# Running sums for neighbour ranks, a 16-bit un-permute, and norms on GpSimd, in a four-layer graph kernel

## The chip, the cores and the metric

One core of one Trainium2 chip runs the whole program in one launch. The metric is device time in microseconds, the median of the runs; less is better. Five engines work side by side, each with its own instruction stream in program order, held together by semaphores: TensorE (PE in the profile, its weight loads PEld), VectorE (DVE), ScalarE (ACT), GpSimd (POOL) and SyncE (SP), which here issues the DMAs of the main part.

## The reference, cut to what matters

There are 32 graphs of 512 nodes with 64 features. Four layers follow each other, and each is `x = layernorm(x + layer(x))`.

```python
x = _layernorm(x + _L0_gnn_ref(x, adj))                       # A x / clip(deg, 1)
x = _layernorm(x + _L1_gnn_ref(x, adj, weight, bias))         # Chebyshev polynomials of the Laplacian, 4 orders
x = _layernorm(x + _L2_gnn_ref(x, adj, att_W, att_b))         # hyperbolic attention over all pairs of nodes
x = _layernorm(x + _L3_gnn_ref(x, adj, nodemask, W1, b1, W2, b2))
```

Layer 3 is what the change touches most. It thins out each node's neighbour list, takes for each node and feature three interpolated quantiles (0.25, 0.5, 0.75) over the node's neighbours, and puts the weighted sum of them through a two-layer perceptron:

```python
vals = jnp.where(valid[..., None], x[:, None, :, :], big)
sv = jnp.sort(vals, axis=2)
for tau, wt in zip(TAUS, QWEIGHTS):
    q = gather(lo) * (1.0 - frac) + gather(hi) * frac         # at rank tau * (m - 1)
    agg = agg + wt * q
y = relu((x + agg) @ W1 + b1) @ W2 + b2
```

`_layernorm` divides by `sqrt(var + 1e-5)` over the 64 features and has no scale or offset of its own.

## The kernel before, in words

A graph's 512 nodes lie on 128 partitions times T = 4 blocks. Each graph passes through lanes, and each lane has its own buffers and PSUM banks (`BANKS`, L513: two for pairs, one for each of the others that it names).

- `front` (L882) loads the adjacency, transposes it to `AT`, and computes layers 0 and 1. The degree gives `deg`, `dc`, `dm`, `dsc` and `pos` (L913 to L932), columns of 128x4 numbers; `dsc` scales every `y` that is multiplied by the adjacency.
- `pairs` (L969) is layer 2's arithmetic over all pairs of nodes; its second half, from L1094, is the lane `tail`, which ends in the norm after layer 2 and in `x3h`, the result split into three bfloat16 parts.
- `stage_graph` (L878) finds the thinned neighbour matrix `V` and then, in `order` (L830), sorts the nodes by their number of neighbours. `rk` is a node's place, `perm` a one-hot matrix of it, and `VP` the permuted neighbour matrix in four blocks. `slot` says which number a neighbour has in a node's list. It is a prefix sum over nodes: block j needs a triangular product with its own block and a product with a matrix of twos for every earlier block, ten products in all. Four more, with ones, give the counts.
- `gather` (L1147) turns slots into one-hot matrices `oh` on VectorE and multiplies them with `x3h`, so that each neighbour's features land in their slot. Before this, GpSimd pads the unused columns of the sorting areas `SB` and `SH` (L1157). `SB` holds the body (nodes with fewer neighbours) and `SH` the head (the 64 nodes of two graphs with most).
- `sort` (L1239) runs a sorting network of minima and maxima over `SB` on VectorE, weights the sorted values and adds them up in the PSUM bank `PA`; `ap` is the result, for two graphs together.
- `head` (L1270) does the same for `SH`, and calls `finish` (L1315) for each graph of a pair. `finish` puts the nodes back in their old order: `PT`, one-hot in fp32, times `ap` in fp32, four products a graph of 64 columns of weights and 512 moving columns. `dense` (L1346) is the perceptron and the last norm. For the last pair, `spots` (L1296) prepares the one-hot matrices beforehand.

Every norm is `layernorm` (L725). VectorE takes statistics of each block (`bn_stats`, then `bn_aggr`) and adds the epsilon, GpSimd raises to the power -0.5 (`rsqrt`, L719), VectorE forms the offset, and ScalarE applies scale and offset.

Nothing runs in the order of the code. The class `Order` (L181) records every operation with an engine, a cost, its buffers and what it depends on; `issue` (L295) then plays the operations through in planned time and writes out one instruction order for each engine. An operation's due time comes from its lane's window in `STAGES` (L1415), in units of one graph's period: a lane with (2.7, 2.9) is due 2.7 periods after the graph's turn. Costs are numbers in the code: a small GpSimd operation counts 1.0 us and 0.5 us until its result is seen (L468), `rsqrt` 0.8 and 0.6 (L722). TensorE stays with one class of matmul shape unless another class is due more than `STAY` = 51 us earlier (L188). Where the plan leaves TensorE idle for more than 0.3 us, it puts in filler matmuls on zeros or on constants (`stay_active`, L1451). Once written, the order is fixed, and an instruction that waits holds all that stands behind it on its engine.

The groups of the profile carry the helper's line: 448 is `tt`, 452 `ts`, 455 `stt`, 458 `cp`, 471 and 475 the GpSimd helpers, 483 `act`, 502 `mm`, 507 `tr`. Tile names carry the lane in front.

Of the kernel before, what the change touches and what calls it, by code (L numbers as in the profile page):

```python
# [8 lines left out]
F32 = mybir.dt.float32  # L9
# [11 lines left out]
P = 128  # L21
EPS = 1e-5
# [158 lines left out]
class Order:  # L181
# [6 lines left out]
    STAY = 51.0  # L188
# [215 lines left out]
def tile_adj_resnorm(ctx: ExitStack, tc: tile.TileContext, x, adj, nodemask, w1k, b1k, att_w, att_b,  # L404
# [61 lines left out]
    def gp(f, out, ins):  # L466

        seq.op("POOL", 1.0, 0.5, f, [out], ins)  # L468
# [142 lines left out]
    onesb = const.tile([P, P], BF16, name="onesb")  # L611
    nc.vector.memset(onesb, 1.0)
    zero = const.tile([P, 2 * P], BF16, name="zero")
# [105 lines left out]
    def rsqrt(v, name):  # L719

        y = col(name)
        seq.op("POOL", 0.8, 0.6, lambda: nc.gpsimd.tensor_tensor(y, v, mhalf, op=OP.pow), [y], [v])  # L722
        return y

    def layernorm(dst, z):  # L725

        st = seq.tile(pools["small"], [P, T, nc.vector.BN_STATS_DIM], F32, "st", 2)
# [102 lines left out]
    def order(b, res):  # L830
# [18 lines left out]
        cp(rkh, rk)  # L849
# [9 lines left out]
        slot = seq.tile(pools["keep"], [P, T, N], F16, "slot", 2)  # L859
        for j in range(T):  # L860
            pt = bank()
            for k in range(j + 1):
                mm(pt, UC[:, :P] if k == j else UC[:, P:2 * P], VP[:, k, :], start=(k == 0), stop=(k == j))
            act(slot[:, j, :], pt, AF.Copy)
        pt = bank()
        for k in range(T):
            mm(pt, onesP, VP[:, k, :], start=(k == 0), stop=(k == T - 1))
# [14 lines left out]
    def front(b, res):  # L882
# [39 lines left out]
        layernorm(R[:, :, :D], z)  # L922
# [3 lines left out]
        ts(dm, deg, 2e-35, None, op0=OP.max)  # L926
        dsc = rsqrt(dm, "dsc")
        pos = col("pos")
        ts(pos, deg, 0.0, None, op0=OP.is_gt)
        tt(dsc, dsc, pos, op=OP.mult)  # L930
# [23 lines left out]
        for t in range(T):  # L954
            mm(pt[:, t, :], onesb, bias1, start=True, stop=False)
            for u in range(nu):
                mm(pt[:, t, :], RT[:, u, t * P:(t + 1) * P], wk[:, u, :], start=False, stop=(u == nu - 1))

        FL = FLS[:, b % 2]
        var, rs = layernorm(FL[:, :, :D], pt[:, :, :D])  # L960
# [8 lines left out]
    def pairs(b, res):  # L969
# [129 lines left out]
        stt(s1, q, -2.0, s1, op0=OP.mult, op1=OP.add)  # L1099
        tt(s1, s1, hh, op=OP.mult)  # L1100
# [169 lines left out]
    def head(b, res):  # L1270
# [21 lines left out]
        act(ap[P - CUT:, :, 1, :], pt[P - CUT:, :2 * P].rearrange("p (g c) -> p g c", g=2), AF.Copy)  # L1292
        for g in range(2):
            finish(b - 1 + g, res["ends"][g], ap[:, g], res["spots"][g] if b == B - 1 else None)

    def spots(ends):  # L1296
# [4 lines left out]
        ones = [seq.tile(mid, [P, 4, N], F32, f"ones{g}", 1, tag) for g, tag in enumerate(("EX", "RW"))]  # L1301
# [13 lines left out]
    def finish(b, end, ap, spot):  # L1315
        rk, x3 = end
        if spot:
            ones, home = spot
            po = bank(home=home and "pairs")
            for u in range(2):  # L1320
                for h in range(2):
                    mm(po[h * D:(h + 1) * D, :], ap[:, u, h * D:(h + 1) * D], ones[:, 2 * h + u], start=(u == 0),
                       stop=(u == 1 and h == 1), pair=True)
# [11 lines left out]
        for u in range(2):  # L1335
            PT = seq.tile(pools["fin"], [P, 2, N], F32, "PT", 1)
            for h in range(2):
                onehot(PT[:, h, :], rr, nposc[:, 2 * h + u:2 * h + u + 1], pools["fin"])
            for h in range(2):
                mm(po[h * D:(h + 1) * D, :], ap[:, u, h * D:(h + 1) * D], PT[:, h, :], start=(u == 0),  # L1340
                   stop=(u == 1 and h == 1), pair=True)
# [4 lines left out]
    def dense(po, x3T, x3, dst, nm, home=None):  # L1346
# [14 lines left out]
        for t in range(T):  # L1361
            mm(py[:, t, :], onesb, bias2, start=True, stop=False)
# [8 lines left out]
    limits = const.tile([B, 2, K + 1], F32, name="limits")  # L1371
# [12 lines left out]
    def within_bounds():  # L1384
# [17 lines left out]
        for i, op in enumerate((OP.is_gt, OP.is_lt)):  # L1402
# [12 lines left out]
    STAGES = {"front": (-0.6, -0.5), "pairs": (1.2, 1.3), "tail": (0.2, 1.5), "graph": (0.9, 1.0), "gather": (2.7, 2.9),  # L1415
              "sort": (4.5, 4.6), "head": (4.7, 5.6), "ends": (4.0, 4.5), "check": (3.4, 4.8)}

    nc.scalar.preload_act_table_set("natural_log_exp_and_others")
    with ExitStack() as fast:
# [31 lines left out]
        def stay_active():  # L1451
            if seq.open:
                return nc.tensor.matmul(PA[:, 2 * P:], zero[:, :P], zero, start=False, stop=False)  # L1453
# [251 lines left out]
```

## Time and profile before

| | |
|---|---|
| median of 3 runs | 2621.71 us (2621.48 to 2628.53) |
| the profiled execution | 2622.02 us, span 2620.2 us |
| mean granted TensorE clock | 0.982 |
| busy: PE, DVE, ACT, POOL | 2458.2, 2402.7, 1879.2, 815.8 us |
| DMA | 49.96 MB, 19 GB/s on average |

The span runs from the first instruction to the last. An engine counts as busy while at least one of its instructions runs, register, semaphore and DMA-issuing instructions left out. A line of a group reads: source line, engine, operation, output and inputs by name, shape, count, then busy time in us and the mean of one in ns, then the idle time ahead of the group's instructions and what ended it. A line of waits reads: who waited, for whom, us in total, times, the longest. Matmuls overlap, and their ends are modelled, so that a TensorE which is 94% busy may still have room.

### The profile page before, as it was taken

What the parts mean: (1) busy time and instruction counts of PE and PEld (TensorE: products, weight loads), DVE (VectorE), ACT (ScalarE), POOL (GpSimd) and SP (SyncE); (2) the same over time, 40 slices, a digit from 0 to 9 for tenths busy, and PEclk for the clock granted to TensorE, in tenths of its full rate; (3) what the DMA queues carried; (4) which work ended last, traced back from release to release, by engine and by line L of the source; (5) the groups of instructions that cost most, each with busy time, mean ns of one, the idle gap of its engine ahead of it and who ended that gap; (6) DMA issues with size and microseconds to landing.
All of it is one profiled execution on the core that took longest, in us unless ns stands there. A gap on an engine that the chain in (4) does not pass through costs nothing.

```text
span 2620.2 us, 55667 instructions
## 1 busy us (share of the span) xinstructions
PE 2458.2 (94%) x19641; PEld 1635.4 (62%) x19667; DVE 2402.7 (92%) x9002; ACT 1879.2 (72%) x4406; POOL 815.8 (31%) x1783
## 2 busy tenths in 40 slices
PE   7999999999999999999999999999999999999997
PEld 6666566666666666666656666566666666666655
DVE  3668998999999999999999999999999999998996
ACT  5666677767777777767777677777777778776761
POOL 1233332332343333322333233333323333332210
PEclk9999999999999999999999899999999999998999
DMA  1100000000000000000000000000000000000000
GB/s 38 33 23 21 17 14 15 25 22 23 18 11 22 20 25 21 24 17 13 20 21 25 19 19 13 20 23 22 26 19 13 18 19 26 19 11 3 5 7 8
DMA packets 119723, 49.96 MB, mean 19 GB/s; under 512 B 53740, under 2 KB 119436, under 8 KB 119436
## 3 DMA queue, kind: packets, MB, share of 16 engines
q1 hardware_dynamic: 118272, 46.15, 6.4%
q8 instruction: 156, 2.56, 0.4%
q14 instruction: 131, 1.07, 0.1%
q10 hardware_dynamic: 1164, 0.18, 0.0%
HBM read 37.93 MB, written 8.39 MB: 18 GB/s over the span
## 4 chain that ended last, share of the span: by engine, by line
DVE 72%; PE 18%; ACT 6%; issue 2%; POOL 2%; DMA 0%; ACTq 0%; DVEq 0%
DVE SB L448 17%; DVE SH L448 8%; DVE gather_oh L452 6%; PE front_bank L502 5%; DVE pairs_Q L448 4%; PE gather_bank L502 3%; PE graph_bank L502 3%; DVE pairs_RW L448 3%; PE pairs_bank L502 3%; DVE sort_prod L448 3%; DVE pairs_Wt L455 3%; DVE pairs_L L455 2%; DVE tail_v L448 2%; DVE pairs_EX L448 2%; DVE pairs_RW L455 2%
## 5 line engine op out<-in xcount | busy, mean ns | idle before, releaser
L448 DVE TENSOR_TENSOR SB<-SB 128x448 f32<-128x448 f32 (+11 forms) x1424 | 565.8, 424 | 12.2 <-ACT SB L483 0.7
L502 PE MATMUL gather_bank<-gather_oh,tail_x3h 128*64 128x448 f16 (+5 forms) x5376 | 516.5, 321 | 4.8 <-ACT SB L483 3.4
L502 PEld LDWEIGHTS <-tail_x3h 128*64 128x64 bf16 x5376 | 296.0, 111 | 214.3 <-issue 112.8
L448 DVE TENSOR_TENSOR SH<-SH 128x32 f32<-128x32 f32 (+11 forms) x1744 | 347.4, 246 | 8.1
L502 PE MATMUL pairs_bank<-pairs_FT 67*128 67x512 f32 (+7 forms) x768 | 316.9, 516 | 18.7 <-ACT pairs_EX L483 7.1
L452 DVE TENSOR_SCALAR gather_oh<-graph_slot 128x256 f16<-128x256 f16 (+9 forms) x864 | 252.3, 337 | 25.3 <-PE gather_bank L502 23.5
L502 PE MATMUL front_bank<-front_AT,front_y 128*64 128x512 f32 x768 | 189.5, 607 | 18.5 <-DVE front_y L448 17.0
L502 PEld LDWEIGHTS pairs_bank<-pairs_FT 67*128 67x128 f32 (+1 forms) x768 | 130.2, 194 | 83.2 <-issue 19.7
L502 PE MATMUL graph_bank<-graph_perm,graph_V 128*128 128x512 f16 x512 | 141.0, 382 | 16.1 <-DVE graph_perm L452 13.8
L502 PEld LDWEIGHTS <-graph_nbT 128*128 128x128 f16 x1536 | 113.1, 99 | 57.6 <-issue 17.3
L722 POOL TENSOR_TENSOR front_rs<-front_var,mhalf 128x4 f32<-128x4 f32 x64 | 83.4, 1303 | 201.8 <-DVE front_var L452 152.9
L502 PEld LDWEIGHTS front_bank<-XA,front_AT 128*128 128x128 f32 x1024 | 126.0, 194 | 13.6 <-issue 6.3
L1453 PE MATMUL PA<-zero 128*128 128x256 bf16 x973 | 132.9, 278 | 0.1
L502 PE MATMUL pairs_bank<-FLS,pairs_Wt 128*128 128x66 f32 x1024 | 124.7, 274 | 3.9 <-DVE pairs_Wt L455 3.8
L502 PEld LDWEIGHTS pairs_bank<-FLS,pairs_Wt 128*128 128x128 f32 x1024 | 120.6, 192 | 10.9 <-DVE pairs_Wt L455 7.8
L502 PE MATMUL front_bank<-XA,front_AT 128*128 128x65 f32 x1024 | 124.5, 274 | 0.0
L448 DVE TENSOR_TENSOR pairs_RW<-pairs_RW,pairs_EX 128x640 f32<-128x640 f32 x128 | 104.1, 815 | 18.7 <-ACT pairs_RW L483 18.4
L502 PEld LDWEIGHTS <-tabs 128*128 128x128 f16 x1296 | 78.3, 100 | 64.2 <-issue 54.9
L502 PEld LDWEIGHTS front_bank<-front_AT,front_y 128*64 128x64 f32 x768 | 54.5, 137 | 95.6 <-issue 63.0
L483 ACT ACTIVATE graph_VP<-graph_bank 128x512 f16<-128x512 f32 x128 | 75.5, 590 | 53.7 <-PE graph_bank L502 49.4
L483 ACT ACTIVATE SB<-gather_bank 128x448 f32<-128x448 f32 (+2 forms) x192 | 81.3, 438 | 43.4 <-PE gather_bank L502 43.0
L502 PE MATMUL head_bank<-head_PT,sort_ap 128*64 128x512 f32 x240 | 111.2, 608 | 0.1
(354 smaller groups left out, 6569.8 us busy)
## 6 DMA issues: line engine op xcount, KB each, us to landing
front_A<-in_adj_dram SPq DMA_DIRECT2D x128, 256.0 KB, 2.7
XA<-in_x_dram SPq DMA_DIRECT2D x32, 128.0 KB, 2.2
xs<-tail_x SPq DMA_DIRECT2D x32, 128.0 KB, 1.9
out_dram<-head_zo SPq DMA_DIRECT2D x31, 128.0 KB, 2.0
out_dram<-tail_ends SPq DMA_DIRECT2D x1, 128.0 KB, 2.1
wk<-in_L_gnn_weight_dram ACTq DMA_DIRECT2D x1, 64.0 KB, 3.0
w1s<-in_L_gnn_W_dram ACTq DMA_DIRECT2D x2, 32.0 KB, 2.0
attw<-in_L_gnn_att_W_dram ACTq DMA_DIRECT2D x2, 0.2 KB, 3.2
```

What stands on the lines that cost most here:

```text
L448: vec(lambda: nc.vector.tensor_tensor(out, a, b, op=op), out, [a, b])
L452: vec(lambda: nc.vector.tensor_scalar(out, a, s1, s2, op0=op0, **kw), out, [a], True, (s1, s2))
L455: vec(lambda: nc.vector.scalar_tensor_tensor(out, a, s, b, op0=op0, op1=op1), out, [a, b], False, (s,))
L483: 0.3, lambda: nc.scalar.activation(out, a, f, scale=scale, **kw), [out, accum_out], [a, after] + sc, table)
L502: return nc.tensor.matmul(out, w, a, start=start, stop=stop)
L722: seq.op("POOL", 0.8, 0.6, lambda: nc.gpsimd.tensor_tensor(y, v, mhalf, op=OP.pow), [y], [v])
L1453: return nc.tensor.matmul(PA[:, 2 * P:], zero[:, :P], zero, start=False, stop=False)
```

## The change

Four things are edited. The prefix sum keeps a running sum of the blocks of `VP` on VectorE, so that each later block needs two products and the counts one. `ap` is split into three bfloat16 parts `aph`, and the one-hot matrices of `finish` and `spots` become half precision. The norms of the lanes tail and head, and small column operations (`rkh`, `dm`, `pos`, `dsc`, `s1`), go to GpSimd; the norms of the front lane keep their form (`soon=True`). The ordering's numbers change: costs of GpSimd operations, `STAY`, `STAGES`. Besides, `onesP` takes the place of `onesb`, the filler on zeros reads its moving operand from one column, and `limits` is half precision.

```diff
-    STAY = 51.0
+    STAY = 70.0
...
-        seq.op("POOL", 1.0, 0.5, f, [out], ins)
+        seq.op("POOL", 0.28, 0.25, f, [out], ins)
...
-    onesb = const.tile([P, P], BF16, name="onesb")
-    nc.vector.memset(onesb, 1.0)
-    zero = const.tile([P, 2 * P], BF16, name="zero")
+    zero = const.tile([P, P], BF16, name="zero")
...
-        seq.op("POOL", 0.8, 0.6, lambda: nc.gpsimd.tensor_tensor(y, v, mhalf, op=OP.pow), [y], [v])
+        seq.op("POOL", 1.1, 0.3, lambda: nc.gpsimd.tensor_tensor(y, v, mhalf, op=OP.pow), [y], [v])
...
-    def layernorm(dst, z):
+    def layernorm(dst, z, soon=False):
+        if not soon:
+            st = seq.tile(pools["small"], [P, T, nc.vector.BN_STATS_DIM], F32, "st", 2)
+            for t in range(T):
+                bn_stats(st[:, t, :], z[:, t, :])
+            off, even, var, d, odd, v = (st[:, :, i] for i in range(6))
+            gtt(d, even, odd, op=OP.subtract)
+            gtt(var, var, v, op=OP.add)
+            gts(d, d, 0.5, None, op0=OP.mult)
+            gts(var, var, 1.0 / D, EPS, op0=OP.mult, op1=OP.add)
+            gtt(d, d, d, op=OP.mult)
+            gtt(v, var, d, op=OP.add)
+            rs = rsqrt(v, "rs")
+            gtt(off, even, odd, op=OP.add)
+            gts(off, off, -0.5, None, op0=OP.mult)
+            gtt(off, off, rs, op=OP.mult)
+            for t in range(T):
+                act(dst[:, t, :], z[:, t, :], AF.Identity, bias=off[:, t:t + 1], scale=rs[:, t:t + 1])
+            return
...
-        cp(rkh, rk)
+        gts(rkh, rk, 1.0, None, op0=OP.mult)
...
+        sums = [None, VP[:, 0, :], seq.tile(gm, [P, N], F16, "sums", 1, "junk"), VP[:, 0, :], VP[:, 1, :]]
         for j in range(T):
             pt = bank()
-            for k in range(j + 1):
-                mm(pt, UC[:, :P] if k == j else UC[:, P:2 * P], VP[:, k, :], start=(k == 0), stop=(k == j))
+            mm(pt, UC[:, :P], VP[:, j, :], start=True, stop=(j == 0))
+            if j:
+                mm(pt, UC[:, P:2 * P], sums[j], start=False, stop=True)
+                tt(sums[j + 1], sums[j], VP[:, j, :], op=OP.add)
             act(slot[:, j, :], pt, AF.Copy)
         pt = bank()
-        for k in range(T):
-            mm(pt, onesP, VP[:, k, :], start=(k == 0), stop=(k == T - 1))
+        mm(pt, onesP, sums[T], start=True, stop=True)
...
-        layernorm(R[:, :, :D], z)
+        layernorm(R[:, :, :D], z, True)
...
-        ts(dm, deg, 2e-35, None, op0=OP.max)
+        gts(dm, deg, 2e-35, None, op0=OP.max)
         dsc = rsqrt(dm, "dsc")
         pos = col("pos")
-        ts(pos, deg, 0.0, None, op0=OP.is_gt)
-        tt(dsc, dsc, pos, op=OP.mult)
+        gts(pos, deg, 0.0, None, op0=OP.is_gt)
+        gtt(dsc, dsc, pos, op=OP.mult)
...
-        stt(s1, q, -2.0, s1, op0=OP.mult, op1=OP.add)
-        tt(s1, s1, hh, op=OP.mult)
+        gts(q, q, -2.0, None, op0=OP.mult)
+        gtt(s1, s1, q, op=OP.add)
+        gtt(s1, s1, hh, op=OP.mult)
...
+        aph = seq.tile(pools["fin"], [P, 3, 2, 2, P], BF16, "aph", 1)
+        for q in range(3):
+            act(aph[:, q], ap, AF.Copy)
+            if q < 2:
+                tt(ap, ap, aph[:, q], op=OP.subtract)
         for g in range(2):
-            finish(b - 1 + g, res["ends"][g], ap[:, g], res["spots"][g] if b == B - 1 else None)
+            finish(b - 1 + g, res["ends"][g], aph[:, :, g], res["spots"][g] if b == B - 1 else None)
...
-            PT = seq.tile(pools["fin"], [P, 2, N], F32, "PT", 1)
+            PT = seq.tile(pools["fin"], [P, 2, N], F16, "PT", 1)
...
-            for h in range(2):
-                mm(po[h * D:(h + 1) * D, :], ap[:, u, h * D:(h + 1) * D], PT[:, h, :], start=(u == 0),
-                   stop=(u == 1 and h == 1), pair=True)
+            for q in range(3):
+                for h in range(2):
+                    mm(po[h * D:(h + 1) * D, :], ap[:, q, u, h * D:(h + 1) * D], PT[:, h, :], start=(u == 0 and q == 0),
+                       stop=(u == 1 and q == 2 and h == 1))
...
-    STAGES = {"front": (-0.6, -0.5), "pairs": (1.2, 1.3), "tail": (0.2, 1.5), "graph": (0.9, 1.0), "gather": (2.7, 2.9),
-              "sort": (4.5, 4.6), "head": (4.7, 5.6), "ends": (4.0, 4.5), "check": (3.4, 4.8)}
+    STAGES = {"front": (-0.6, -0.4), "pairs": (0.7, 1.4), "tail": (0.3, 1.9), "graph": (0.9, 1.1), "gather": (2.7, 2.9),
+              "sort": (4.6, 4.7), "head": (4.7, 6.2), "ends": (4.3, 4.4), "check": (3.4, 4.9)}
...
-                return nc.tensor.matmul(PA[:, 2 * P:], zero[:, :P], zero, start=False, stop=False)
+                return nc.tensor.matmul(PA[:, 2 * P:], zero, zero[:, 0:1].to_broadcast([P, 2 * P]), start=False, stop=False)
```

More of the change, by code (lines that the diff above doesn't have):

```diff
@@ L954, in front @@
         for t in range(T):
-            mm(pt[:, t, :], onesb, bias1, start=True, stop=False)
+            mm(pt[:, t, :], onesP, bias1, start=True, stop=False)
             for u in range(nu):
@@ L959, in front @@
         FL = FLS[:, b % 2]
-        var, rs = layernorm(FL[:, :, :D], pt[:, :, :D])
+        var, rs = layernorm(FL[:, :, :D], pt[:, :, :D], True)
         tt(FL[:, :, D + 2:D + 7:4], pt[:, :, D:], bc(rs, 2), op=OP.mult)
@@ L1300, in spots @@
         home = seq.tile(mid, [P, 4, N], F32, "ends", 1, "Q")
-        ones = [seq.tile(mid, [P, 4, N], F32, f"ones{g}", 1, tag) for g, tag in enumerate(("EX", "RW"))]
+        ones = [seq.tile(mid, [P, 4, N], F16, f"ones{g}", 1, tag) for g, tag in enumerate(("EX", "RW"))]
         seq.lane = "tail"
@@ L1320, in finish @@
             for u in range(2):
-                for h in range(2):
-                    mm(po[h * D:(h + 1) * D, :], ap[:, u, h * D:(h + 1) * D], ones[:, 2 * h + u], start=(u == 0),
-                       stop=(u == 1 and h == 1), pair=True)
+                for q in range(3):
+                    for h in range(2):
+                        mm(po[h * D:(h + 1) * D, :], ap[:, q, u, h * D:(h + 1) * D], ones[:, 2 * h + u],
+                           start=(u == 0 and q == 0), stop=(u == 1 and q == 2 and h == 1))
             for t in range(T):
@@ L1335, in finish @@
         for u in range(2):
-            PT = seq.tile(pools["fin"], [P, 2, N], F32, "PT", 1)
+            PT = seq.tile(pools["fin"], [P, 2, N], F16, "PT", 1)
             for h in range(2):
                 onehot(PT[:, h, :], rr, nposc[:, 2 * h + u:2 * h + u + 1], pools["fin"])
-            for h in range(2):
-                mm(po[h * D:(h + 1) * D, :], ap[:, u, h * D:(h + 1) * D], PT[:, h, :], start=(u == 0),
-                   stop=(u == 1 and h == 1), pair=True)
+            for q in range(3):
+                for h in range(2):
+                    mm(po[h * D:(h + 1) * D, :], ap[:, q, u, h * D:(h + 1) * D], PT[:, h, :], start=(u == 0 and q == 0),
+                       stop=(u == 1 and q == 2 and h == 1))
         for t in range(T):
@@ L1361, in dense @@
         for t in range(T):
-            mm(py[:, t, :], onesb, bias2, start=True, stop=False)
+            mm(py[:, t, :], onesP, bias2, start=True, stop=False)
             mm(py[:, t, :], hT[:, t * P:(t + 1) * P], w2s, start=False, stop=True)
@@ L1370, in tile_adj_resnorm @@
     flag = const.tile([1, 1], I32, name="flag")
-    limits = const.tile([B, 2, K + 1], F32, name="limits")
+    limits = const.tile([B, 2, K + 1], F16, name="limits")
     for s in range(K + 1):
```

## The prediction

> **What bounds the kernel now.** I read the page's first part and its chain of waits, then busy time by stretches of the span, then VectorE's waits, then the groups kept apart by shape, last the timeline for what one instruction really occupies.
>
> ```profile
> PE 2458.2 (94%) x19641; PEld 1635.4 (62%) x19667; DVE 2402.7 (92%) x9002; ACT 1879.2 (72%) x4406; POOL 815.8 (31%) x1783
> ...
> DVE 72%; PE 18%; ACT 6%; issue 2%; POOL 2%; DMA 0%; ACTq 0%; DVEq 0%
> ```
>
> Two engines are full, and the chain that ended last runs over VectorE for 72% and TensorE for 18%. The stretches say how full they are once the pipeline of graphs has filled:
>
> ```profile
> 0.00:80.00 80.00, 65.83 (x529) 51.30 (x529) 30.36 (x153) 43.99 (x78) 14.53 (x100) 1.00 0.16 44
> 80.00:160.00 80.00, 75.98 (x530) 51.56 (x529) 54.23 (x170) 57.21 (x130) 21.84 (x58) 1.00 0.06 18
> ...
> 1200.00:1600.00 400.00, 381.93 (x2977) 248.25 (x2979) 380.42 (x1452) 304.36 (x710) 131.00 (x274) 0.98 0.07 20
> ```
>
> Columns: length, then busy time of PE, PEld, DVE, ACT, POOL. The five stretches from 400 to 2400 us leave VectorE idle for 18.7, 19.1, 19.6, 17.5 and 11.1 us: 86 of 2000 us, 4.3%. TensorE is idle there for 102 us, 5.1%. Graph 2's norm after layer 2 begins at 316 us and graph 28's at 2319: 77.0 us a graph, in which VectorE has 3.3 us left. What ends VectorE's idle time is mostly a matmul:
>
> ```profile
> DVE gather_oh L452 <- PE gather_bank L502: 23.5, 18, 3.0
> ...
> DVE front_st L714 <- PE front_bank L502: 17.1, 32, 3.7
> DVE front_q L448 <- PE front_bank L502: 13.2, 6, 4.5
> ...
> DVE head_off L455 <- POOL head_rs L722: 4.0, 5, 1.1
> ```
>
> With front_deg 10.2, pairs_EX 9.3 and pairs_L 7.6, six waits for TensorE make 81 us. So VectorE's work is the floor, and TensorE's promptness decides how far above it the kernel stands.
>
> The rows that price the change:
>
> ```profile
> L502 PE MATMUL graph_bank<-graph_VP,UC 128*128 128x512 f16 x320 | 91.2, 383 | 2.6 <-ACT graph_VP L483 1.9 <-ACT graph_slot L483 0.5
> L502 PE MATMUL head_bank<-head_PT,sort_ap 128*64 128x512 f32 x240 | 111.2, 608 | 0.1
> L448 DVE TENSOR_TENSOR graph_nbT<-graph_nbT,identb 128x512 f16<-128x512 f16 x32 | 13.2, 414 | 0.1
> L717 DVE BATCH_NORM_AGGREGATE tail_mv<-tail_st 128x2 f32<-128x6 f32 x128 | 11.5, 150 | 0.0
> L722 POOL TENSOR_TENSOR tail_rs<-tail_var,mhalf 128x4 f32<-128x4 f32 x32 | 48.4, 1512 | 146.5 <-DVE tail_var L452 146.5
> L471 POOL TENSOR_TENSOR pairs_sn<-pairs_sn,FLS 128x4 f32<-128x4 f32 x32 | 11.1, 346 | 1.7
> L1157 POOL MEMSET SB<- 128x10 f32 (+2 forms) x96 | 13.3, 143 | 278.1 <-DVE SB L448 263.6 <-ACT SB L483 14.4
> ```
>
> A mean overstates what an instruction occupies when others queue behind it, for they overlap. The timeline shows it:
>
> ```profile
> 1620.93 0.36 DVE L717 BATCH_NORM_AGGREGATE tail_mv<-tail_st 128x2 f32<-128x6 f32 x4
> 1621.21 0.19 DVE L452 TENSOR_SCALAR gather_oh<-graph_slot 128x256 f16<-128x256 f16 x1
> ```
>
> Four aggregates of 150 ns each, and the next instruction starts 0.28 us after the first: 70 ns apiece. I price by start to start (medians over the trace): 70 ns for a small VectorE operation, 335 ns for a half-precision tensor_tensor of 512, 600 ns for one with fp32 in it, 216 ns for a 512-column f16 matmul. Busy time by count of a row is the other bound.
>
> **What the Trainium skill says.** "VectorE: DVE Perf Modes" (Mode 2×_1P) gives tensor_tensor two results a cycle only with 16-bit data; the trace agrees: 414 ns for 512 f16, and 415 ns for half as many fp32. So the sums go at the fast rate, the subtraction from fp32 does not. "GPSIMD Engine Reference" (section 8) says that GpSimd shares its SBUF interfaces with VectorE and contends with two-input instructions. In this trace VectorE does not pay: the 128x448 exchanges of SB average 616 ns where GpSimd was idle for over nine tenths of them (182) and 618 ns where it was busy for over six tenths (126). "TensorE: Matmul & The Clock Gate" (Part 3) lets matmuls in different column groups run together; the gather's 448-column products of 64 columns start 115 ns apart on average, where 216 x 448/512 = 189 would be serial.
>
> **The change part by part.** Counts come from the built instruction lists of both kernels.
>
> Running sums. Slot products go from 320 to 224, count products from 128 to 32: 192 fewer. At 216 ns that is 41 us; by busy time over count (91.2/320 = 285 ns, and 33.1/128 = 259 for the counts) it is 52; I take -45 on TensorE. It adds 3 additions a graph on VectorE, 96 x 335 ns = +32 us. New waits: product j=2, j=3 and the count wait for an addition. The graph lane has one PSUM bank, so each already waits for the 588 ns eviction of slot by ScalarE, which covers a 335 ns addition that VectorE issues at once. If VectorE is late by more than 0.25 us, TensorE's in-order queue, other lanes' gathers and pairs included, stands behind it.
>
> Un-permuting in parts. The 120 fp32 products (240 records, mean 346 ns start to start) cost 83 us. They become 360 of 64x512 in 16-bit: 131 ns each if always beside the other column half (115 x 512/448), 216 if never: 47 to 78 us. In the built order 179 of the 360 have such a neighbour, so 62: -21 us, bounds -36 and -5. The last pair's 8 become 24: -1. VectorE gets two subtractions a pair, 32 x 600 ns = +19 us; ScalarE three copies, 48 x 0.62 us (726 ns at 640) = +30. Copies and subtractions are a chain of some 4 us before the un-permuting; only the output follows, so the other lanes hide it, except for the last pair, where it adds about 4 us to the end, less about 1 for the shorter products.
>
> Norms. In tail and head, 64 norms lose 4 aggregates, the epsilon and the offset on VectorE: 384 x 70 ns = -27 us, and the 5.7 us that VectorE waited for head_rs and tail_rs. GpSimd gets 9 more instructions a norm: 576 x 0.35 us = +200. A norm's latency grows by about 3 us. After tail comes gather, due most of a graph later, which hides that; at the end of the kernel it is +2 us.
>
> Small operations. rkh, dm, pos, dsc and two for s1: 192 x 71 ns = -14 us on VectorE; 224 x 0.35 = +78 on GpSimd, which goes from 816 to about 1,095 us. No DMA moves, and GpSimd issues none.
>
> Free edits: fillers of another form and onesP for onesb (28 ns either way). The order has 62 more fillers: +7 us of TensorE in its gaps. It also has 18 more loads of activation tables at 1.28 us: +23 on ScalarE, to 1,932, still under 75%. I cost the table loads at nothing because ScalarE stands under VectorE and TensorE; without that cover they cost up to 23 us. New due times and class stickiness reorder everything; the profile prices neither, and I bound them by -30 and +30 us.
>
> Sums: **TensorE -60** (bounds -96 to -38); **VectorE** +32 +19 -27 -14 -6 = **+4** (about -45 if each small operation were worth its row's 150 ns, +10 if the waits stay). So the floor does not move, and the gain must come from VectorE's idle time. TensorE's free share rises from 5.1% by 60/32 = 1.9 us of 77 (2.4%) to 7.5%. If waits go as one over the free share, 86 us shrinks by 86 x (1 - 5.1/7.5) = 28. That is my choice and the softest step. -28 +4 = -24, end and start cancelling within 5 us: from the profiled execution's 2622.0 (span 2620.2, 1.8 around it, 0.3 above the median of the runs) to **2598**.
>
> **Rivals.**
> A second gain: the new order also removes waits on ScalarE and between lanes, and two thirds of the 86 us go: -57 +4, about **2569**. For it: 94% and 92% busy still leave 86 us. Against: 60 us less TensorE is all that the profile promises.
> No change: the lanes wait for their own chains (matmul, eviction, VectorE), not for a busy TensorE, and the saved time turns into TensorE idle: +4, minus a few, **2622**. For it: the chain gives TensorE 18% only, and 60/2458 of that is 11 us.
> Slower: GpSimd's in-order queue. Its padding of SB (L1157) waits for the previous sort, 263.6 us in 65 waits, up to 17.9. Behind it now stand also dm, dsc, the head's norm and s1, on which front_y and tail_v on VectorE depend. In the built order the next instruction after a padding is front_rs 21 times, head_st 16, tail_s1 13. If VectorE loses more than 24/32 = 0.75 us a graph to that, the gain is gone; at 1.5 us more than that, **2646**. Against it: front and tail run well ahead of what uses them, and today VectorE waits for GpSimd for some 10 us in all.
> That the change does not do what it says is no rival: the lists show every count.
>
> **Chances.** 2598 has 0.45, 2569 0.19, no change 0.13, slower 0.23. About 0.3%, 8 us, is what a measurement of this kernel can tell from none. The range 2550 to 2645 takes in both gains, no change and half of the slow case. Most of the chance lies on one side; the likeliest case alone spans 2580 to 2614.
>
> **What would show it.** Right: TensorE with 192 slot and count products less and more idle time from 400 to 2400 us; VectorE's waits on front_bank and gather_bank down; VectorE busy within 25 us of 2403 and its share above 92.5%; GpSimd near 42%. Wrong: VectorE idle after POOL lines above 40 us (the queue), or 4.3% idle unchanged from 400 to 2400 us (no conversion), or VectorE's busy time up by over 25 us (the additions mispriced).

## The result and the profile after

The changed kernel takes **2725.7 us** (median of 4 runs, 2717.2 to 2733.5); the kernel before, on the same chip, 2624.8. The ratio is 1.038 (95% interval 1.034 to 1.043): about 101 us slower, where 24 us faster was forecast, and outside the forecast range. The profiled execution took 2733.5 us, of which the span is 2731.8.

The first part of the page of the changed kernel (busy time and share of the span of each engine):

```profile
PE 2480.6 (91%) x19665; PEld 1687.5 (62%) x19665; DVE 2415.5 (88%) x8553; ACT 1916.4 (70%) x4472; POOL 1103.8 (40%) x2583
```

The floor hardly rose: VectorE has 12.8 us more work than before, GpSimd stands where it was expected, at 1,104 us. What rose is the time in which VectorE does nothing. The stretches of the changed kernel (length, then PE, PEld, DVE, ACT, POOL, granted clock), one of the five from 400 to 2400 us and the sum of the five:

```profile
1200.00:1600.00 400.00, 363.16 (x2790) 243.15 (x2790) 355.58 (x1229) 281.95 (x663) 173.22 (x372) 0.91 0.07 19
...
sum 2000.00, PE 1832.19 PEld 1233.61 DVE 1839.85 ACT 1459.52 POOL 867.97; mean PE 366.44 PEld 246.72 DVE 367.97 ACT 291.90 POOL 173.59
```

2000 - 1839.85 is 160 us of idle VectorE, where it was 86; TensorE is idle for 168 us, before 102. From graph 2 to graph 28 the norm after layer 2 starts every 80.5 us in place of every 77.0; 3.5 us over 32 graphs are 112 us, by which the two profiled spans differ too (2731.8 and 2620.2 us).

Now the waits of each engine in the changed kernel (engine and line, what it waited for, then us in total, times, longest). ScalarE first:

```profile
ACT tail_x L483 <- POOL tail_st L471: 118.5, 30, 7.3
...
ACT head_zo L483 <- POOL head_st L471: 30.6, 9, 12.6
```

TensorE's, which were 0.5 and 1.3 us before:

```profile
PE graph_bank L502 <- ACT graph_slot L483: 45.8, 17, 5.5
...
PE front_bank L502 <- ACT front_sums L483: 23.2, 14, 4.7
```

VectorE's:

```profile
DVE tail_rem L448 <- ACT tail_x3h L483: 49.2, 21, 4.6
```

These waits hang together. In the kernel before ScalarE waited 35.5 us for tail's offset, on VectorE, 3.8 us at most. Now it waits 118.5 us for tail_st, the norm's statistics, whose small operations are on GpSimd. ScalarE takes its instructions in order, so the evictions of the graph lane's one bank (graph_slot) and of the front lane's (front_sums) stand behind that wait, and TensorE stands behind them. VectorE's 49.2 us, a wait that the kernel before does not have, lie on the norm's own path: tail_rem forms the second part of x3h and needs the scaled norm, and what follows on VectorE stands behind it. The timeline of the changed kernel shows one such case (start, length, then what; in brackets the idle time before and what ended it):

```profile
2151.44 6.83 POOL L471 TENSOR_TENSOR tail_st<-tail_st 128x4 f32<-128x4 f32 x3 [1.99 <-DVE tail_st L712]
...
2161.20 0.77 ACT L483 ACTIVATE tail_x<-tail_v,tail_st,tail_rs 128x64 f32<-128x64 f32 x2 [6.20 <-POOL tail_st L471]
2161.88 0.57 ACT L483 ACTIVATE graph_slot<-graph_bank 128x512 f16<-128x512 f32 x1
...
2162.50 1.01 PE L502 MATMUL graph_bank<-graph_VP,UC 128*128 128x512 f16 x2 [5.28 <-ACT graph_slot L483]
```

Three GpSimd instructions of four columns take 6.83 us. ScalarE waits 6.20 us; then it needs 0.57 us for the eviction that TensorE has waited 5.28 us for. VectorE ends its last instruction at 2159.2 and finds nothing more to do. From 2155 to 2163 us TensorE is busy for 2.72 of 8 us, VectorE for 4.23.

The gaps may cost TensorE more than their length. The clock records of the trace have it at half rate for 326 us in 45 stretches, 3.4 to 20.5 us each, where the kernel before had 97 us in 14. "TensorE: Matmul & The Clock Gate" in the Trainium skill (Part 1) says that the clock falls to half after an idle window of about 3.4 us and comes back after a busy one. The trace agrees with the window's length: nearly all stretches are whole multiples of 3.4 us. It does not agree that the window must be idle: ahead of the 14 stretches of the kernel before, TensorE was busy, by the profile, for 45 to 87% of the last 3.4 us, with no gap over 1.9 us. Matmuls at the half rate fit with TensorE's busy time having risen by 22 us although it has 192 slot and count products less. How much of the loss is theirs was not measured by itself.

The groups of the changed kernel say what the norm's small instructions take (count, then busy us and mean ns):

```profile
L471 POOL TENSOR_TENSOR tail_st<-tail_st 128x4 f32<-128x4 f32 x160 | 137.6, 879 | 104.0 <-DVE tail_st L712 99.4 <-DVE graph_rk L452 2.4
...
L475 POOL TENSOR_SCALAR tail_st<-tail_st 128x4 f32<-128x4 f32 x96 | 50.7, 528 | 7.8
```

The forecast priced them at 350 ns and the planner at 280. The median of the first row is 275 ns, but a tenth of them take over 2.9 us and the longest 6.9. From the end of the last bn_stats to ScalarE's first use of the norm, 8.0 us pass on average; before it was 3.2.

And what comes after the norm? In the trace of the kernel before, the gather of a graph follows its tail at once (the scaling, the first part of x3h, the first product that reads it):

```profile
1307.54 1.43 ACT L483 ACTIVATE tail_x<-tail_v,tail_off,tail_rs 128x64 f32<-128x64 f32 x4 [1.37 <-DVE tail_off L455]
...
1310.34 0.41 ACT L483 ACTIVATE tail_x3h<-tail_x 128x256 bf16<-128x256 f32 x1
...
1311.73 0.30 PE L502 MATMUL gather_bank<-gather_oh,tail_x3h 128*64 128x256 f16 x2
```

In 24 of the 32 graphs that product starts before the last of the three parts is done. In the changed kernel there is a little room: it starts 5.1 us after the last part on average, and before it in 9 graphs.

### The profile page after: what moved, and what is told of

It reads as the page before. It is cut to its first block, busy times and chain, and to the rows that moved or that the text cites. A ratio compares the mean times of both kernels' runs of the same rounds, so it can differ in the third digit from the quotient of the medians.

```text
span 2731.8 us, 56146 instructions
## 1 busy us (share of the span) xinstructions
PE 2480.6 (91%) x19665; PEld 1687.5 (62%) x19665; DVE 2415.5 (88%) x8553; ACT 1916.4 (70%) x4472; POOL 1103.8 (40%) x2583
## 5 line engine op out<-in xcount | busy, mean ns | idle before, releaser
L448 DVE TENSOR_TENSOR SB<-SB 128x52 f32<-128x52 f32 (+11 forms) x1424 | 566.2, 425 | 14.7 <-ACT SB L483 1.7
L502 PEld LDWEIGHTS <-tail_x3h 128*64 128x64 bf16 x5376 | 307.2, 114 | 203.7 <-issue 98.4
L448 DVE TENSOR_TENSOR SH<-SH 128x128 f32<-128x128 f32 (+11 forms) x1744 | 347.9, 246 | 7.7
L502 PE MATMUL pairs_bank<-pairs_FT 67*128 67x512 f32 (+7 forms) x768 | 339.1, 548 | 14.9 <-DVE pairs_EX L455 4.9
L471 POOL TENSOR_TENSOR tail_st<-tail_st 128x4 f32<-128x4 f32 x160 | 137.6, 879 | 104.0 <-DVE tail_st L712 99.4
L502 PEld LDWEIGHTS <-graph_nbT 128*128 128x128 f16 x1536 | 117.8, 100 | 85.9 <-issue 39.5
L502 PE MATMUL pairs_bank<-FLS,pairs_Wt 128*128 128x66 f32 x1024 | 133.1, 281 | 1.2 <-DVE pairs_Wt L455 1.2
L483 ACT ACTIVATE tail_x<-tail_v,tail_st,tail_rs 128x64 f32<-128x64 f32 x128 | 47.2, 429 | 118.5 <-POOL tail_st L471 118.5
L471 POOL TENSOR_TENSOR head_st<-head_st 128x4 f32<-128x4 f32 x160 | 49.6, 327 | 199.2 <-DVE head_st L712 195.0
L502 PE MATMUL front_bank<-fold,front_sums 128*128 128x64 f32 x768 | 107.8, 283 | 23.5 <-ACT front_sums L483 23.2
L502 PEld LDWEIGHTS front_bank<-fold,front_sums 128*128 128x128 f32 x768 | 104.9, 202 | 39.0 <-ACT front_sums L483 28.7
```

Source lines behind the costliest of these rows:

```text
L448: vec(lambda: nc.vector.tensor_tensor(out, a, b, op=op), out, [a, b])
L471: gp(lambda: nc.gpsimd.tensor_tensor(out, a, b, op=op), out, [a, b])
L483: 0.3, lambda: nc.scalar.activation(out, a, f, scale=scale, **kw), [out, accum_out], [a, after] + sc, table)
L502: return nc.tensor.matmul(out, w, a, start=start, stop=stop)
```

## Experiments

Theory A: the loss is the tail's norm, in which ScalarE stands in order behind slow small instructions on GpSimd. Theory B: the new due times and prices are to blame. Each ratio below is to the kernel before on the same chip, with its 95% interval.

**The norms on VectorE again**, in tail alone, in head alone, in both. In all three the norm's small tiles of tail and head rotate through one buffer in place of two, which makes room.

```diff
-        layernorm(x3, v)
+        layernorm(x3, v, True)
```

> The changed kernel with the norm after layer 2 (tail) back on VectorE, one buffer for its small tiles; the rest of the change and the new numbers stay. Theory A (the tail norm on GpSimd is starved by VectorE's long instructions, ScalarE stands in order behind it with PSUM evictions, TensorE waits and falls to half clock): most of the 101 us comes back, 2625 to 2655; ScalarE's wait of tail_x for POOL tail_st (118.5 us) is gone, half-clock time falls from about 326 to under 180 us. Theory B (the new ordering numbers): no more than 20 us comes back, 2705 to 2725. Theory C (running sums make TensorE wait for additions): the same, about 2725.

> The changed kernel with the last norm (head) back on VectorE, the tail norm still on GpSimd. Theory A: nothing but a reordering comes of it, 2695 to 2740, and ScalarE's wait of tail_x for POOL stays near 118 us. A variant of A in which any norm on GpSimd costs alike: half comes back, about 2670. Theories B and C: about 2725.

> The changed kernel with both moved norms (tail and head) back on VectorE, one buffer for their small tiles; running sums, 16-bit un-permute and the column operations on GpSimd stay. Theory A: like the kernel with the tail norm back alone (2644) within 25 us, VectorE's busy time up by another 10 us. If the rest of the change is a gain that the norms ate: below 2600. If the running sums or the column operations cost on their own: still 2630 to 2660.

Tail: 2644.5 us, ratio 1.009 (1.005 to 1.012), as theory A said. Head: 2755.9, 1.050 (1.045 to 1.055), above every range given for it. Both: 2677.2, 1.024 (1.021 to 1.026), 33 us above the tail's norm alone where 25 was the most expected. The sum of the same stretches, for the tail's norm back:

```profile
sum 2000.00, PE 1852.12 PEld 1256.19 DVE 1913.57 ACT 1504.04 POOL 756.94; mean PE 370.42 PEld 251.24 DVE 382.71 ACT 300.81 POOL 151.39
```

VectorE is idle for 86 us, as before the change, although the operations stay otherwise changed. TensorE's waits in this kernel:

```profile
PE graph_bank L502 <- ACT graph_slot L483: 7.3, 10, 1.4
...
PE front_bank L502 <- ACT front_sums L483: 4.4, 4, 1.8
```

They were 45.8 and 23.2 us. The half rate falls from 326 to 146 us. This one part undone takes 80 of the 101 us back and nearly all of these waits with them; VectorE's wait at tail_rem is down to 1.9 us. The head's norm gives nothing back: with it alone on VectorE, ScalarE still waits 105.9 us for tail_st, and the new order is 30 us worse.

**Due times and prices.** The changed operations with the numbers of before, and the other way round.

```diff
-    STAGES = {"front": (-0.6, -0.4), "pairs": (0.7, 1.4), "tail": (0.3, 1.9), ...
+    STAGES = {"front": (-0.6, -0.5), "pairs": (1.2, 1.3), "tail": (0.2, 1.5), ...
```

> All the moved and changed operations of the changed kernel, ordered with the numbers of before (stickiness 51, old windows, GpSimd costs 1.0/0.5 and 0.8/0.6). Theory B: most of the 101 us comes back, 2620 to 2650. Theory A: part of it, since the old cost of 1.5 us an instruction places ScalarE's part of the norm later in ScalarE's order, 2640 to 2690. Theory C: about 2720.

> The kernel before, its operations untouched, ordered with the changed kernel's numbers (stickiness 70, new windows, cheap GpSimd costs). Theory B (the numbers alone do the harm): near the changed kernel, 2690 to 2740. Theory A: no norm of nine GpSimd instructions is there to be starved, so no such loss, 2600 to 2670; reordering alone moves the time by up to 40 us either way, as the head norm's return did (+30).

> The changed kernel with the tail's norm on VectorE and with the due times, stickiness and planned GpSimd costs of the kernel before. Theory A (ScalarE, in order, behind GpSimd's norm in the tail is the loss; the numbers act by themselves): without that norm the old numbers do no harm, 2600 to 2650 us, and since the new numbers cost 44 us on the old operations it may come below the kernel before, 2619. Rival B (the numbers belong to the new operations, and the old ones make a poor order with them whatever the norm does): 2680 us or more, with VectorE's wait for the gather's bank above 50 us.

The changed kernel with the old numbers: 2767.6 us, 1.056 (1.051 to 1.061). The kernel before with the new ones: 2662.6, 1.016 (1.013 to 1.019). The tail's norm back and the old numbers: 2688.4, 1.027 (1.023 to 1.030). So B falls as a single cause, since the old numbers make the changed kernel worse, but it has a part: the new numbers on the old operations cost 44 us. Theory A missed too: it hoped for 2640 to 2690 us in the first of these kernels and for 2650 or less in the third, where the rival's 2680 or more came true (VectorE's wait for the gather's bank, over 50 us by the rival, was 46.1).

The first and the third differ in the tail's norm alone, and by 79 us, as much as with the new numbers. Yet ScalarE waits only 2.6 us for tail_st in the first. VectorE's wait for the gather, with the norm on GpSimd and with it on VectorE:

```profile
DVE gather_oh L452 <- PE gather_bank L502: 85.0, 49, 11.0
```

```profile
DVE gather_oh L452 <- PE gather_bank L502: 46.1, 41, 2.9
```

In both the gather starts right behind its tail (before the last part of x3h in 26 and in 30 of the 32 graphs). With the norm on GpSimd, 14.2 us pass from bn_stats to the norm's first use in place of 3.6, and the pause from one graph's last gather product to the next graph's first is 32.8 us on average (graphs 3 to 29) in place of 21.1. That fits a second road by which the same norm costs as much: its length, where the gather has no slack. No run separates it from the new order that comes with it.

**The norm planned at what it takes.** Same work, same engines; only the planner is told that the nine small GpSimd operations of the tail's norm and of the head's take 0.9 us each in place of 0.28.

```diff
-        seq.op("POOL", 0.28, 0.25, f, [out], ins)
+        seq.op("POOL", price[0], 0.25, f, [out], ins)
...
+            price[0] = 0.9
...
+            price[0] = 0.28
```

> The changed kernel with the same work on every engine; only the planned cost of the nine small GpSimd instructions of the tail and head norms goes from 0.28 to 0.9 us (which is what tail_st took on average), so that ScalarE's normalisation stands later in ScalarE's order. Theory A: the wait of tail_x for POOL falls from 118.5 us to under 40 and most of the time comes back, 2630 to 2670. Theory B (windows and stickiness) and theory C: 2705 to 2735.

2671.0 us, ratio 1.019 (1.014 to 1.024), a microsecond above theory A's range: 55 us come back with no operation moved to another engine. Its tail_st instructions are as slow as ever (807 ns on average in the larger row, 6.9 us at most), and the norm takes even longer, 10.9 us from bn_stats to its first use in place of 8.0. But ScalarE's wait for it is nearly gone:

```profile
ACT tail_x L485 <- POOL tail_st L473: 12.4, 4, 6.6
```

With the higher price the planner places ScalarE's use of the norm later: 14 other ScalarE instructions stand on average between the statistics and the scaling, in place of 5. TensorE's two waits for ScalarE fall to 0.8 and 3.1 us, VectorE's at tail_rem to 5.7. So **about half of the loss goes with the engines standing still for the norm, though the norm itself grew longer.** The other half is not explained by these waits: this kernel still has 259 us of half rate, and it is 26 us slower than the one with the tail's norm on VectorE.

The same price for the head's norm, in the kernel with the tail's norm back:

> The changed kernel with the tail's norm on VectorE, and the head's norm on GpSimd planned at 0.9 us for each of its nine small instructions in place of 0.28. Theory A (what is left of the loss is the head's norm coming later than planned): 2610 to 2635 us against 2644 for the norm back alone. Rival (the 25 us left are the order's other marks, not the price): 2640 us or more.

2656.6 us, 1.012 (1.010 to 1.015), against 2644.5 without it, as the rival said. A price of the head's norm that is too low is not the 25 us that are left.

**The tail's norm alone, in the kernel before.**

```diff
+        if not soon:
...
+            gtt(d, even, odd, op=OP.subtract)
...
+            gtt(off, off, rs, op=OP.mult)
...
+            return
```

This is the changed kernel's layernorm; front, pairs and head call it with soon=True, so tail alone takes the new branch.

> The kernel before with one part of the change: the tail's norm on GpSimd (32 norms, nine small instructions each), planned at the 1.0 us that every small GpSimd operation has there. Theory A (ScalarE held behind a norm that comes later than planned): at this price the planner puts it late enough, so within 25 us of 2619, with ScalarE's wait for tail_st below 40 us. Rival (any norm on GpSimd in the tail costs as much as in the changed kernel): 2680 us or more.

> The same, with those nine instructions alone planned at 0.28 us, as in the changed kernel. Theory A: ScalarE waits for tail_st by 60 us or more and TensorE is at half clock for over 180 us, against 97 before; 2660 to 2720 us. Rival (the loss needs the other parts or the new due times): within 20 us of the run with the price of 1.0.

At the price of 1.0: 2660.9 us, 1.016 (1.012 to 1.020), with 0.9 us of waiting for tail_st. At 0.28: 2637.6 us, 1.006 (1.002 to 1.009). Theory A was wrong on both. The first should have come within 25 us and lost 40 with next to no wait; there, 13.6 us pass before the norm's first use, and VectorE waits 36.7 us for the gather's bank in place of 23.5. For the second it said 2660 to 2720: the wait is there, but smaller, and the half rate is 117 us, not over 180. The rival's 20 us between the two came out as 23. ScalarE's wait and the GpSimd group of the second kernel:

```profile
ACT tail_x L485 <- POOL tail_st L473: 35.4, 19, 3.9
```

```profile
L473 POOL TENSOR_TENSOR tail_st<-tail_st 128x4 f32<-128x4 f32 x160 | 69.3, 453 | 137.8 <-DVE tail_st L716 129.8 <-DVE front_var L452 5.9
```

The same 160 instructions take 453 ns on average here and 879 in the changed kernel. So the same norm costs 80 us in the changed kernel's order and 17 or 40 in the order of before. The dearer price here costs more, without a wait for the norm: the remedy of one order is not that of another.

**How far orders scatter.** A lane's stickiness 69 in place of 70.

```diff
-    STAY = 70.0
+    STAY = 69.0
```

> The changed kernel with the stickiness of a lane at 69 in place of 70: the same operations in a slightly other order. Theory A: the norm is still priced at a third of what it takes, so ScalarE still waits for GpSimd's tail_st by 60 to 140 us, TensorE is at half clock for over 230 us, and the time is 2690 to 2760 us. Rival (the loss is an accident of this one order): below 2680 us, with ScalarE's wait below 50 us.

2710.0 us, 1.036 (1.032 to 1.039), ScalarE's wait for tail_st 94.4 us, half rate 203 us (expected over 230). The changed kernel's ratio was 1.038 (1.034 to 1.043): the intervals overlap, and this reordering moved the time by no more than the runs can tell. Others move it further: the two sets of numbers by 42 us on the changed kernel's operations and by 44 on those of before, and undoing the sums, below, by 61. The 80 us of the tail's norm came twice, with the new numbers and with the old; the head norm's 30 and the 12 of its price are not to be read closely.

**The running sums and the un-permuting.** Sums undone in the kernel with the tail's norm back; sums alone in the kernel before; sums and un-permuting in parts in the kernel before.

```diff
+            mm(pt, UC[:, :P], VP[:, j, :], start=True, stop=(j == 0))
+            if j:
+                mm(pt, UC[:, P:2 * P], sums[j], start=False, stop=True)
+                tt(sums[j + 1], sums[j], VP[:, j, :], op=OP.add)
```

> The changed kernel with the tail's norm on VectorE and the running sums undone: 192 more slot and count products, 96 additions less. Step 'running sums' of the prediction: TensorE's busy time up by 40 to 55 us from 2411, VectorE's down by some 32 from 2426, and since both engines are near full, the time within 15 us of 2644 either way. Rival C (the additions' waits hold TensorE's in-order queue, and the rest of the loss of 25 us lies there): 2625 us or less, with TensorE's waits for graph_bank lower by 10 us or more.

> The kernel before with the running sums alone, and its own due times. The prediction's step: TensorE's busy time down by about 45 us from 2458, VectorE's up by about 32 from 2403, and as VectorE is the floor, no gain: 2610 to 2650 us. Rival (as undoing the sums in the other kernel suggests, fewer products between the graph lane's evictions are worth more than the additions cost): 2600 us or less, and VectorE idle less than 86 us from 400 to 2400 us.

> The kernel before with the running sums and the un-permuting in bfloat16 parts (with the filler's other form and shorter rotation of the norm's small tiles in tail and head, which make room for it), no norm and no small operation moved to GpSimd, and the due times of before. The prediction's steps add up to TensorE -60 and VectorE +51: if VectorE's floor decides, 2640 to 2680 us. Rival (TensorE's saving decides): 2600 us or less, which would beat both kernels.

Undone: 2705.9 us, 1.032 (1.028 to 1.036), 61 us worse than with them; neither expectation held. TensorE's busy time rose by 102 us (40 to 55 were expected), it is at half rate for 287 us, and VectorE is idle for 158 of the same 2000 us, as much as in the changed kernel, though the tail's norm is on VectorE here. What causes that was not found; an order can lose as much without a norm on GpSimd in the tail. Alone in the kernel before: 2625.5 us over 20 runs, 1.0023 (1.0008 to 1.0039), within the 2610 to 2650 that the forecast's step gave. The page of the latter:

```profile
PE 2442.8 (93%) x19718; PEld 1642.4 (62%) x19741; DVE 2431.3 (92%) x9098; ACT 1872.5 (71%) x4398; POOL 813.7 (31%) x1783
```

VectorE has 28.6 us more, where 32 was forecast. TensorE has only 15.4 less; its fillers grew from 1,081 to 1,347 and from 147 to 183 us of busy time, so without them it has 51 less, where 45 was forecast. The saving went into fillers and idle time, VectorE's idle time fell from 86 to 73 us, and the added work of VectorE took that and a little more. In the order of before, VectorE is the floor, and the sums do not pay.

With the un-permuting in parts as well, 2701.8 us, 1.030 (1.027 to 1.032), above both expectations and 76 us more than with the sums alone. VectorE's longest wait there:

```profile
DVE gather_oh L452 <- PE gather_bank L502: 74.1, 41, 4.7
```

Before it was 23.5; this kernel has 2,066 fillers (277 us). Whether the parts themselves or the order that the old due times make of them is at fault was not told apart; the same wait stands first in the other two kernels with the parts and the old numbers. No kernel tried here beats the kernel before.

**Why a GpSimd instruction lasts 7 us.** In the changed kernel the long ones begin beside a row of VectorE's SBUF-only instructions without a gap. Of the eight longest, which span the starts of 8 to 12 VectorE instructions each, six end some 0.15 us after VectorE starts an instruction that reads PSUM (five times front_q, once sort_prod), and one as VectorE runs out of work. "GPSIMD Engine Reference" in the Trainium skill (section 8) says that GpSimd shares its SBUF interfaces with VectorE and contends with instructions that have two SBUF inputs and with those in a two-port mode. One change of layout (the four columns of a statistic side by side in place of six apart) and three kernels of VectorE streams with GpSimd beside them:

```diff
-            st = seq.tile(pools["small"], [P, T, nc.vector.BN_STATS_DIM], F32, "st", 2)
+            st = seq.tile(pools["small"], [P, nc.vector.BN_STATS_DIM, T], F32, "st", 2)
```

> The changed kernel with the statistics of the moved norms laid out so that GpSimd reads four adjacent numbers instead of four with a step of six; nothing else differs. If the step makes GpSimd's instructions long: tail_st falls from 0.70 us on average (up to 6.9) to about 0.35, and most of the time comes back, 2630 to 2670. If only the coincidence with VectorE's long instructions does (theory A as stated): tail_st stays at 0.6 to 0.8 us and the time at 2700 to 2745.

> None of the network is computed; the outputs are zeros. Nine phases one after the other: in each, GpSimd runs 12 additions of 128x4 fp32 (six on columns of adjacent numbers, flat; six with a step of 6, as the norm reads its statistics), while VectorE runs back to back one kind of instruction: none, two-input 128x640 fp32 (tt, stt), 128x640 fp32 with one input (ts), 2x224 two-input as in the sort (two), 128x1792 f16 with one input (oh), PSUM input (psum), 128x32 (small), and the mix of the pairs lane. Theory A (GpSimd waits for the memory interface while long VectorE instructions hold it): an addition takes 0.2 us alone and 1 us or more beside tt, stt or the mix, with gaps only where VectorE pauses; small leaves it near 0.3. If the step of the operand is what costs: step takes several times flat, also in the phase with no VectorE work. If neither: 0.2 to 0.4 us in all phases.

> Nothing of the network is computed here; the output is zeros. Twelve dependent GpSimd operations of 128x4 fp32 (two adds, then a multiplication by a constant) run beside streams of VectorE work that is issued without a gap: none; 128x640 fp32 in place on four tiles (own) and on one (same); 128x448 f16 with two inputs (f16); 128x256 fp32 (mid); bn_stats of 64 (bn); a 640 and an f16 one in turn (pair); the kernel's row of unlike instructions (row), and that row with an instruction on PSUM at every sixth place (rowps). Theory: unlike instructions or in-place ones shut GpSimd out over several of VectorE's instructions, as in the kernel: in row, own or same a 128x4 operation takes over 1.5 us on average and some take 4 us; in rowps about half of row. Rival: VectorE alone lets GpSimd in at each boundary of two instructions: no phase above 0.75 us on average and none of the operations above 1.5 us; then the 4 to 7 us of the kernel need something else beside VectorE.

> Nothing of the network is computed here; the output is zeros. Twelve dependent GpSimd operations of 128x4 fp32 beside VectorE's 128x640 in-place stream alone (own), with ScalarE copying 128x640 in SBUF (ownact), copying from PSUM (ownacp), with a stream of TensorE matmuls (ownpe), with both (ownall, and rowall with the row of unlike instructions), and beside ScalarE (act) or TensorE (pe) without VectorE. Theory: the other engines' traffic is what holds a GpSimd instruction past several of VectorE's: in ownact, ownpe or ownall some take over 1.5 us, where own alone gives 0.65. Rival: ScalarE and TensorE make no difference, all within 0.1 us of own; then what holds it in the kernel stays open.

The layout changes nothing: 2718.1 us, 1.040 (1.036 to 1.045), ScalarE's wait 117.8. The small kernels show a contention that goes one way. The groups of the first (GpSimd alone, beside 128x640 fp32 with two inputs, beside 128x512 with one input in PSUM), and VectorE's row:

```profile
L78 POOL TENSOR_TENSOR step_none<-step_none 128x4 f32<-128x4 f32 x6 | 1.2, 202 | 0.4
...
L78 POOL TENSOR_TENSOR step_tt<-step_tt 128x4 f32<-128x4 f32 x6 | 4.1, 678 | 0.4
...
L78 POOL TENSOR_TENSOR step_psum<-step_psum 128x4 f32<-128x4 f32 x6 | 1.2, 202 | 0.4
...
L43 DVE TENSOR_TENSOR dstc<-srca,srcb 128x640 f32<-128x640 f32 x20 | 16.2, 811 | 0.0
```

It looks as if GpSimd's addition waits out one instruction of VectorE's: it lasts 0.13 us less than one, here (0.68 against 0.81 us) as beside two fp32 inputs of 448 (0.48 against 0.61) and one of 640 (0.35 against 0.48). VectorE's instructions take 814 ns on average beside an addition and 811 without one. The page's first kind is thus seen, 0.68 beside two fp32 inputs against 0.20 beside bn_stats; which instructions are in a two-port mode no run here shows. The second adds in-place and mixed streams, the third ScalarE and TensorE beside them (ownall has both):

```profile
L99 POOL TENSOR_TENSOR flat_row<-flat_row 128x4 f32<-128x4 f32 x8 | 5.1, 632 | 22.8 <-DVE flat_row L91 22.2
```

```profile
L124 POOL TENSOR_TENSOR flat_ownall<-flat_ownall 128x4 f32<-128x4 f32 x8 | 5.2, 652 | 24.9 <-DVE flat_ownall L110 24.4
```

No GpSimd instruction took over 0.8 us in any of the three, so their theories of 1 us and of 1.5 us were wrong and the rivals held, but for one phase of the second at 0.77 us where 0.75 was the limit. What shuts GpSimd out over 8 to 12 of VectorE's instructions in the kernel stays open; it is not the step of the columns, not in-place or mixed work as such, not ScalarE's or TensorE's traffic. That it is the same contention is argued from where the long ones end, not shown.

## Why the prediction was wrong, point by point

- **Running sums**: sizes right where they were run alone (TensorE -45 forecast, -51 before fillers, -37 by the busy time of the slot and count rows themselves; VectorE +32, +28.6). The waits that were feared do not show: nothing waits for an addition in the changed kernel's list of TensorE's waits.
- **Un-permuting in parts**: TensorE's row went from 111.2 to 86.0 us of busy time, -25 for a forecast -21, which went by starts. The forecast's 115 ns from one gather product to the next counts pauses of up to 1.5 us; without them it is 97. The chain of copies and subtractions did not show as a wait of any size in the changed kernel.
- **Small operations**: VectorE waits for GpSimd for 17.5 us in all. The rival "GpSimd's in-order queue" had the right sign and the wrong place: the padding of SB waits 266.0 us as before, and VectorE hardly waits behind it.
- **Norms: the step that failed.** "A norm's latency grows by about 3 us. After tail comes gather, due most of a graph later, which hides that." The latency grew by 4.8 us, from 3.2 to 8.0, no great miss. The failure is the second sentence, in two ways. It takes due times for times: in the trace of the kernel before, the gather starts right behind its tail, before the last part of x3h is done in 24 of 32 graphs, so there was hardly any slack to hide in. And it asks who needs the result, not who stands in the queue behind the one that needs it. ScalarE's scaling (tail_x) waits 118.5 us at the head of an in-order engine at 70%, whose share was taken for slack, and graph_slot and front_sums behind it each hold a lane that has one bank. Taking this norm back to VectorE was worth 80 us; planning it dearer, which ends the wait, 55. Every rival and the list of what would show it looked for a wait of VectorE on GpSimd; the waits were ScalarE's on GpSimd and VectorE's on ScalarE. The price of 350 ns an instruction, from a row of 346, was near the median (275) and 2.5 times too low on the mean of the row of 160.
- **Idle time**: the softest step, 86 us shrinking by 28. It grew by 74. TensorE's free share did rise, from 5.1 to 8.4%, but as gaps, 69 us of them in its two waits for ScalarE. Even without the norm on GpSimd, with the sums alone, 86 went to 73 while VectorE's work grew by 28.6.
- **New due times**: bounded by -30 and +30 us; on the old operations they cost 44, outside the bound.
- **Sums**: two results do not follow from their terms. TensorE's bounds come to -82 and -40 us, not -96 and -38; and 2646 is the slow case with 1.5 us a graph in all, not 1.5 on top of 0.75, which would be 2670. Neither bears on the outcome.

The parts do not add up by themselves: new numbers alone +44, the tail's norm alone +17, the sums alone +6; the un-permuting, the head's norm and the small operations were not run alone. In the changed kernel the tail's norm is worth 80, of which some 55 go with the waits for it; the rest of the way is open. That its due time puts it beside VectorE's densest work, which makes its instructions twice as slow, fits the two means (453 and 879 ns) but was not tried by itself. The 25 us left with the tail's norm back are not settled; orders differ by more than that for other reasons.

## What to carry to other kernels

When a step moves to a slower engine, list what stands behind its consumer in the consumer's in-order queue, and which one-buffer lanes those entries serve; an engine at 70% is no slack for that. Read from the trace when the next user really starts; a due time is a wish. A planner that is told 0.28 us for an instruction that takes 0.2 to 7 put its user too early here; compare mean and longest, not the median, of such a row with the planned price. And price a reorder first: here the due times and prices alone moved the same operations by 42 and 44 us.

## What the runs showed of the hardware

- A 128x4 GpSimd addition takes 0.20 us alone; beside VectorE 0.68 with two fp32 inputs of 640, 0.48 with two of 448, 0.35 with one of 640, and 0.20 again where one of VectorE's inputs is in PSUM. VectorE is hardly slowed (814 against 811 ns).
- In the full kernel the same kind of instruction took up to 6.9 us, which no stream of VectorE instructions reproduced; six of the eight longest ended 0.15 us after VectorE started an instruction that reads PSUM.
- 69 us in two of TensorE's waits on ScalarE, up to 5.5 us each, came with 229 us more at half rate. With the norm planned dearer the two waits were 4 us and the half rate still 259, so these waits are not its only source.
- The half rate came in stretches of 3.4 us or multiples of it, also after windows in which TensorE was busy for 45 to 87%, with no gap over 1.9 us (the kernel before).
